# Turning the expert pairs' rows with VectorE's 32x32 blocks in place of TensorE transposes

## The chip, the cores and the metric

The kernel runs on one core of a Trainium2 chip. The metric is the device time of one execution in microseconds (us), as the median of three runs. One execution is also profiled; the profile gives each engine's instructions, waits and transfers. The engines are TensorE (PE, with its weight loads shown as PEld), VectorE (DVE), ScalarE (ACT), GpSimd (POOL) and SyncE (SP, which here only issues transfers).

## What is computed

The input is x, 64 batches of 256 rows with 256 columns, and a 256 x 256 adjacency mask that all batches share. Everything is fp32. Two layers follow one another:

```python
# layer 0
x = x + gat4(layernorm(x), adj, W0, a0)             # 4 heads of 64, softmax over masked neighbours, elu
x = x + layernorm(x) @ weight.T + bias
# layer 1
x = x + gat1(layernorm(x), adj, W1, a1)             # 1 head of 256, relu
t = layernorm(x)                                    # the expert layer gets t and also starts from it
out = t
for e in range(8):                                  # the two best of 8 experts have weights, others 0
    out = out + combine[:, e:e+1] * (gelu(t @ w1[e] + b1[e]) @ w2[e] + b2[e])
x = x + out
```

The router (softmax over 8 logits, the best two, weights made to sum to 1) makes `combine`.

## The kernel before

**Tiling.** A batch is two tiles of 128 rows. Each batch passes through 19 stages (`batch_layers`): attention of layer 0, its linear layer, attention of layer 1, the norm, and the router's logits. A matmul needs the features of its input on the partitions. So the input x is loaded twice: as rows (`xin`) and, for the first projection, as blocks (`xblk`, `load_blocks`) in such an order that one VectorE instruction, which turns every 32x32 block by itself, gives x transposed (line 472). Four transfers load one batch's blocks, one for each group of 32 partitions, in pieces of 32 columns (128 B).

**Experts.** For 62 of the 64 batches ("routed") only the two chosen experts are computed. After the router, `route` computes for each row and choice a place in a buffer in DRAM, `xs`, where every expert has a region; `send` (line 845) scatters the rows there with indirect transfers of GpSimd. A sent row has 260 numbers: 256 features, and 4 more that say to which row of the output it belongs, its first expert, and two numbers for its weight. Full groups of 256 rows of one expert are called pairs (two tiles). `expert_pair` handles one: it loads the rows (`xr`, line 703, one transfer of 128 pieces of 2,080 B) and the expert's first weights (`we`, line 714), turns the rows with four TensorE transposes (`px`, line 721), copies them from PSUM with ScalarE (`sT`, line 725), casts the output row's index to an integer (`to`, line 728) and makes the weight (`w`, lines 730 and 734). `hidden` is the first matmul and the gelu (`ph`, line 753; `hT`, line 759), `result` the second (`py`, line 768; `y`, line 774). ScalarE multiplies by the weight (line 746), and `scatter` (line 785) adds the rows to the output with two indirect transfers of GpSimd, each pair's behind those of the pair before. There are 131 pairs. The last two batches ("dense") get all eight experts.

**Order.** The program order on every engine is the order in which the Python code emits instructions; each engine works through its own instructions in that order. The code emits in steps. Three steps, called phases 0, 1 and 2 in the code, make one period, in which one new batch begins, so six or seven batches are in work at different stages. Every job (a batch, a pair, a scatter) is a generator. It emits one piece per step, and the number that it yields is the rank of its next piece: within a step, pieces are emitted by rising rank. A negative rank means a later place in the same step. In these texts "phase 2 of 3" or "second phase" is the step in which a period's pairs are turned (the code's phase 1), and the third phase is the one after it, in which the next batch begins. Around the change the pieces are:

| step | rank | piece |
|---|---|---|
| second phase | 20, 28 | first projection `pq` (line 365), scaled `q` (line 381) |
| | 25 | `pd`, `z` of layer 1 (lines 419, 424) |
| | 50 | attention of layer 0: `pv` (line 456), `rinv` (463), `hp` (491) |
| | 55 | `pt` of the normed rows (line 351) |
| | 60 | `x2 + rel` and its norm statistics (lines 537, 336, 337); the pair's `px`, `sT`, `to`, `w` |
| | 70 | `pf` (line 511), x2 (line 517) and its norm statistics |
| | 90 | for chunks of one or two batches: places of the rows (lines 880 to 907) |
| third phase | 5 | x1 (lines 500 to 503) |
| | 10 | `pd`, `z` of two heads (lines 435, 442) |
| | 30 | the pair's `hidden`: `ph` |
| | 35, 40 | logits `pl`; attention of layer 1 `pv` |

Batches are routed in chunks of four, later of two and one (`CHUNKS`). Two pairs begin per period on average while batches still come, and three at the end; in the chunks of four the counts go 3, 2, 2, 1. A pair's rows are loaded when the last row of its chunk has been sent.

All these loads are issued by SP in program order. PSUM is used as eight banks in turn (`bank`); `px` takes one for each pair.

Of the kernel before, what the change touches and what calls it, by code (L numbers as in the profile page):

```python
# [9 lines left out]
F32 = mybir.dt.float32  # L10
# [17 lines left out]
def kernel(  # L28
# [72 lines left out]
    def load_blocks(b):  # L101


        t = io.tile([P, KT, N], F32, tag="xblk", name=f"xblk_{b}", bufs=3)
        for g in range(P // S):
            nc.sync.dma_start(
                out=t[g * S : (g + 1) * S].rearrange("q k (c a) -> q k c a", a=S),
                in_=x[b].rearrange("(c q) (k g a) -> g q k c a", q=S, g=P // S, a=S)[g],
            )
        return t  # L110

    S = 32
    AHEAD, BLOCKS_AHEAD = 3, 2
# [40 lines left out]
    def gnn_weights(w, a, heads, slope, name):  # L154

        d = D // heads
        wx = const.tile([P, KT, heads, d + 3], F32, tag=name, name=name)
        for k in range(KT):
            nc.sync.dma_start(
                out=wx[:, k, :, :d],
                in_=w[k * P : (k + 1) * P, :].rearrange("p (h d) -> p h d", h=heads),
            )
        av = work.tile([P, 2, d], F32, tag="e", name=name + "_a", bufs=1)
        nc.scalar.dma_start(out=av.rearrange("p s d -> p (s d)"), in_=rows_to_all(a, 2 * d))
        flat = wx.rearrange("p k h c -> p k (h c)")  # L170
        return flat, lambda: score_columns(wx, av, heads, slope, name)
# [51 lines left out]
    def prepare_r():  # L223
        pr = bank("pr", [KT, E])
        for k in range(KT):
            nc.tensor.transpose(pr[:, k, :], r_in[:, k * P : (k + 1) * P], ident[:E, :E])
        nc.vector.tensor_copy(rT, pr)
# [9 lines left out]
    def pack_expert(e):  # L237
# [4 lines left out]
            in_=w1[e].rearrange("(k p) f -> p k f", p=P),  # L242
# [20 lines left out]
        fill[:, :, D : D + 1], pattern=[[1, 2], [1, 1]], base=(B - 1) * N, channel_multiplier=2,  # L263
        allow_small_or_imprecise_dtypes=True,
# [82 lines left out]
    def transposed(src, tag="xT", bufs=4):  # L347
        pt = bank("pt", [KT, N])
        for t in range(NT):
            for k in range(KT):  # L350
                nc.tensor.transpose(  # L351
                    pt[:, k, t * P : (t + 1) * P], src[:, t, k * P : (k + 1) * P], ident
                )
        dst = work.tile([P, KT, N], F32, tag=tag, name="xT", bufs=bufs)
        nc.scalar.copy(dst, pt)  # L355
        return dst
# [109 lines left out]
    def batch_layers(b, c0, xng, lg):  # L466
# [4 lines left out]
        xT = work.tile([P, KT, N], F32, tag="xT", name="xT", bufs=4)  # L471
        nc.vector.transpose(xT.rearrange("p k n -> p (k n)"), xb.rearrange("p k n -> p (k n)"))
# [99 lines left out]
        xT = transposed(xe[:, :, :D], *(("xTd", DENSE) if dense else ()))  # L572
# [115 lines left out]
    def expert_pair(j, n, ids, ef, regs, needs):  # L688
# [3 lines left out]
        if i == 0:  # L692
# [9 lines left out]
        xr = io.tile([P, 2, ROW], F32, tag="xr", name="xr", bufs=XBUFS)  # L702
        load = nc.sync.dma_start(
            out=xr,
            in_=xs_d.rearrange("(t p k) c -> t p k c", p=P, k=2)[
                bass.ds(t_sp, 1), :, :, :
            ].rearrange("t p k c -> (t p) k c"),
        )
        tc.add_to_no_dep_group("rows", load.ins)
        for name in needs:  # L710
            tc.add_manual_dep(load.ins, name, AFTER, reason="any sent row may lie in the pair")
# [5 lines left out]
        yield 60  # L717
        px = bank("px", [KT, PAIR])
        for t in range(2):
            for k in range(KT):  # L720
                nc.tensor.transpose(  # L721
                    px[:, k, t * P : (t + 1) * P], xr[:, t, k * P : (k + 1) * P], ident
                )
        xT = work.tile([P, KT, PAIR], F32, tag="sT", name="sT", bufs=3)
        nc.scalar.copy(xT, px)  # L725

        to = small.tile([P, 2], I32, tag="to", name="to", bufs=8)
        nc.vector.tensor_copy(to[:, :, None], xr[:, :, D : D + 1])  # L728
        w = small.tile([P, 2], F32, tag="w", name="w", bufs=8)
        nc.vector.scalar_tensor_tensor(  # L730
            w[:, :, None], xr[:, :, D + 1 : D + 2], ef[:, j : j + 1], xr[:, :, D + 2 : D + 3],
            op0=ALU.is_equal, op1=ALU.mult,
        )
        nc.vector.tensor_tensor(w[:, :, None], w[:, :, None], xr[:, :, D + 3 : D + 4], ALU.add)  # L734
        yield 30
        hT = hidden(xT, we)
# [10 lines left out]
        scatters.append((y, to))  # L747
# [31 lines left out]
    def scatter():  # L779

        y, to = scatters.pop(0)
        before = added[-2:] + based
        based.clear()
        for t in range(2):
            d = nc.gpsimd.indirect_dma_start(  # L785
                out=out_rows, out_offset=bass.IndirectOffsetOnAxis(ap=to[:, t : t + 1], axis=0),
# [75 lines left out]
    def route(c, row0, nt, n, last, xng, lg):  # L862
# [46 lines left out]
        r4 = rt([nt, 4], "r4")  # L909
        vec.tensor_scalar(r4[:, :, 0:1], token[:, :nt, None], float(row0), None, op0=ALU.add)  # L910
        vec.tensor_scalar(r4[:, :, 1:2], first[:, :, None], float(E), None, op0=ALU.add)
        two = two_weights(c, nt, ed)
        for k in range(2):
            vec.tensor_copy(r4[:, :, 2 + k : 3 + k], two[:, k, :, None])
        for i, xe in enumerate(xng):
            vec.tensor_copy(xe[:, :, D:], r4[:, i * NT : (i + 1) * NT, :])
# [169 lines left out]
```

## Time and profile before

| | |
|---|---|
| median of three runs | 1705.36 us (1704.01 to 1710.16) |
| profiled execution | 1703.31 us |
| its span, first to last instruction | 1701.6 us |
| mean granted TensorE clock | 0.966 |
| DMA packets | 272,541, of which 153,848 under 512 B |
| issued by SP: `xr` | 131 transfers of 260 KB |
| `we` | 147 of 288 KB |
| `xblk` | 256 of 64 KB |

Of a group of instructions the profile gives its line in the kernel, engine and operation, what is written and read, the count, then the engine's busy time and the mean duration of one, then the idle time of the engine just before such instructions and what ended it. A matmul's duration contains its pipeline; successive ones overlap, so the distance of their starts is what they cost. The idle time of an engine matters only where others wait for it.

### The profile page before, as it was taken

How to read it: one execution, taken by the hardware profiler on the slowest of the kernel's cores; microseconds unless marked ns; L12 is line 12 of the kernel's file. 1: busy time of each engine (PE TensorE's matmuls, PEld its weight loads, DVE VectorE, ACT ScalarE, POOL GpSimd, SP SyncE). 2: the span in 40 equal slices, each digit the busy share in tenths (PEclk: the TensorE clock that was granted, in tenths of full speed). 3: DMA queues.
4: the chain of work that ended last, by engine and by line, in shares of the span. 5: the costliest groups of instructions: out<-in, count | busy, mean ns of one | idle time of the engine just before them, and what ended most of it. 6: DMA issues, size and time to landing. Idle time of an engine off the chain costs nothing. (4 is left out here: it accounts for less than half of the span.)

```text
span 1701.6 us, 29737 instructions
## 1 busy us (share of the span) xinstructions
PE 1536.7 (90%) x8998; PEld 1352.9 (80%) x8998; DVE 1273.9 (75%) x4744; ACT 897.3 (53%) x1965; POOL 879.4 (52%) x790
## 2 busy tenths in 40 slices
PE   5898888899999999999999999999999997698792
PEld 4777777788888888888888888888888886587681
DVE  6888999988878888888888888878889977422221
ACT  0253434465666566656666665655556675433240
POOL 0122334446565665656565656565675656634444
PEclk8999999999999999999999999999999999889896
DMA  4822223345556564646565554555464555674653
GB/s 107 221 51 48 63 75 88 87 131 108 145 127 151 127 152 113 141 107 143 131 142 137 116 148 99 142 124 148 113 140 116 119 142 139 170 196 97 153 124 43
DMA packets 272541, 209.67 MB, mean 123 GB/s; under 512 B 153848, under 2 KB 226560, under 8 KB 272384
## 3 DMA queue, kind: packets, MB, share of 16 engines
q1 hardware_dynamic: 221760, 139.40, 29.6%
q0 software_dynamic: 49632, 67.39, 21.7%
q8 instruction: 74, 1.21, 0.3%
q10 hardware_dynamic: 992, 0.99, 0.2%
q14 instruction: 83, 0.68, 0.1%
HBM read 118.55 MB, written 89.15 MB: 122 GB/s over the span
## 5 line engine op out<-in xcount | busy, mean ns | idle before, releaser
L785 POOL DMA_INDIRECT out_dram<-y,to x262 | 416.2, 1589 | 318.9 <-DMA out_dram<-y,to 145.9
L456 PE MATMUL pv<-q,z 128*128 128x65 f32 (+1 forms) x2560 | 367.4, 298 | 3.6 <-issue 3.0
L456 PEld LDWEIGHTS pv<-q,z 128*128 128x128 f32 x2560 | 330.4, 193 | 15.5 <-issue 3.2
L344 POOL TENSOR_SCALAR rstd<-mv 128x4 f32<-128x4 f32 (+1 forms) x132 | 74.4, 564 | 415.9 <-DVE mv L337 314.4
L753 PE MATMUL ph<-sT,we 128*128 128x256 f32 x1048 | 248.7, 393 | 41.5 <-ACT sT L725 21.8
L845 POOL DMA_INDIRECT xs<-xng,pos x248 | 249.5, 1006 | 69.2 <-issue 67.1
L768 PE MATMUL py<-w2s,hT 128*128 (+1 forms) x1176 | 263.8, 379 | 0.5 <-PE pt L351 0.5
L753 PEld LDWEIGHTS ph<-sT,we 128*128 128x128 f32 x1048 | 202.4, 198 | 71.7 <-ACT sT L725 23.7
L768 PEld LDWEIGHTS py<-w2s,hT 128*128 128x128 f32 x1176 | 219.6, 190 | 28.6 <-PE pt L351 0.7
L355 ACT COPY xT<-pt 128x512 f32<-128x512 f32 x192 | 113.2, 590 | 234.4 <-PE pt L351 228.7
L774 DVE TENSOR_TENSOR y<-py,b2s 128x512 f32<-128x512 f32 x147 | 98.0, 689 | 162.1 <-PE py L768 101.6
L442 DVE SCALAR_TENSOR_TENSOR z<-pd,q,mask 128x256 f32<-128x256 f32 x512 | 211.2, 474 | 0.3 <-PE pd L435 0.2
L759 ACT ACTIVATE hT<-ph,we 128x256 f32<-128x256 f32 x294 | 123.5, 471 | 149.1 <-PE ph L753 101.0
L345 POOL TENSOR_TENSOR rstd<-rstd,mhalf 128x4 f32<-128x4 f32 (+1 forms) x132 | 160.2, 1214 | 11.0
L746 ACT ACTIVATE y<-y,w 128x256 f32<-128x256 f32 x262 | 113.0, 503 | 90.0 <-DVE y L774 86.7
L336 DVE BATCH_NORM_STATS2 stats<-x 128x6 f32<-128x256 f32 x384 | 156.4, 407 | 2.2
L365 PE MATMUL pq<-wx,xT 128*128 128x268 f32 x512 | 137.4, 414 | 8.3 <-DVE wt L239 4.2
L400 PE MATMUL pq<-wx,xT 128*128 128x259 f32 x512 | 129.2, 394 | 16.1 <-ACT xT L355 14.7
L400 PEld LDWEIGHTS pq<-wx,xT 128*128 128x128 f32 x512 | 91.9, 189 | 42.8 <-ACT xT L355 28.7
L365 PEld LDWEIGHTS pq<-wx,xT 128*128 128x128 f32 x512 | 100.8, 201 | 29.4 <-issue 6.9
L511 PE MATMUL pf<-wfT,xT 128*128 128x256 f32 x512 | 122.4, 382 | 1.0 <-issue 0.8
L533 ACT ACTIVATE rel<-pv,rinv 128x256 f32<-128x256 f32 x128 | 53.9, 474 | 110.9 <-DVE rinv L463 107.4
(155 smaller groups left out, 2393.4 us busy)
## 6 DMA issues: line engine op xcount, KB each, us to landing
we<-wpack SPq DMA_DIRECT2D x147, 288.0 KB
xr<-xs SPq DMA_DIRECT2D x131, 260.0 KB
xblk<-in_x_dram SPq DMA_DIRECT2D x256, 64.0 KB
xin<-in_x_dram SPq DMA_DIRECT2D x64, 256.0 KB
out_dram<-base SPq DMA_DIRECT2D x64, 256.0 KB
out_dram<-y,to POOLq DMA_INDIRECT x262
xs<-xng,pos POOLq DMA_INDIRECT x248
xs<-fill SPq DMA_DIRECT2D x9, 260.0 KB
```

Source lines behind the costliest of these rows:

```text
L336: nc.vector.bn_stats(stats[:, t, :], src[:, t, :])
L345: nc.gpsimd.tensor_tensor(rstd[:, :n], rstd[:, :n], mhalf[:, :n], ALU.pow)
L365: nc.tensor.matmul(pq.rearrange("p h c -> p (h c)"), xT[:, k, t * P : (t + 1) * P], wx[:, k, :], start=(k == 0), stop=(k == KT - 1),)
L400: nc.tensor.matmul(pq, xT[:, k, t * P : (t + 1) * P], wx1[:, k, :], start=(k == 0), stop=(k == KT - 1),)
L442: nc.vector.scalar_tensor_tensor(z[:, j, :], pd[:, i, :], q[:, j, h, d + 2 : d + 3], mask[:, j, :], op0=ALU.max, op1=ALU.mult,)
L456: nc.tensor.matmul(pv[:, h, :], z[:, j, t * P : (t + 1) * P], q[:, j, h, : d + 1], start=(j == 0), stop=(j == NT - 1),)
L511: nc.tensor.matmul(pf[:, t, :], xT[:, k, t * P : (t + 1) * P], wfT[:, k, :], start=(k == 0), stop=(k == KT - 1),)
L753: nc.tensor.matmul(ph[:, f, :], we[:, k * D + f * P : k * D + (f + 1) * P], xT[:, k, :], start=(k == 0), stop=(k == KT - 1),)
L759: nc.scalar.activation(hT[:, f, :], ph[:, f, :], AF.Gelu, bias=we[:, C_B1 + f : C_B1 + f + 1])
L768: nc.tensor.matmul(py[:, t, :], hT[:, f, t * P : (t + 1) * P], w2s[:, e, f * D : (f + 1) * D].rearrange("p e c -> p (e c)"), start=(f == 0 ...
L785: d = nc.gpsimd.indirect_dma_start(out=out_rows, out_offset=bass.IndirectOffsetOnAxis(ap=to[:, t : t + 1], axis=0), in_=y[:, t, :], in_off ...
L845: d = nc.gpsimd.indirect_dma_start(out=xs_d[: E * CAP * PAIR, :], out_offset=bass.IndirectOffsetOnAxis(ap=at, axis=0), in_=xe, in_offset=None,
```

## The change

The rows of `xs` are loaded as blocks too. Feature f no longer lies at partition f mod 128 of half f div 128: partition p now holds the features 2p and 2p + 1. So a group of 32 partitions gets 64 neighbouring columns (256 B) of each row; VectorE's turn then reads every second number. The same order of features is used for the input's blocks and for the router's input, and the rows of the weights `W0`, the router and `w1` are loaded to match.

For each pair SP issues five transfers in place of one: four of 32 rows x 8 pieces of 256 B, and a fifth for the four extra numbers of each row, into a tile `xt` of its own with 12 buffers. The piece with the `px` transposes, the ScalarE copy, the cast and `w` at rank 60 is gone. In its place, at rank 95 of the same step, stands one VectorE turn (`turned`); `w` is made behind `hidden`, at rank 65 of the next step. The index of the output row is now stored as an integer when the row is made, so the cast isn't needed; that takes one small instruction per batch in `route`.

```diff
-        t = io.tile([P, KT, N], F32, tag="xblk", name=f"xblk_{b}", bufs=3)
+        t = io.tile([P, N // S, KT * S], F32, tag="xblk", name=f"xblk_{b}", bufs=3)
         for g in range(P // S):
             nc.sync.dma_start(
-                out=t[g * S : (g + 1) * S].rearrange("q k (c a) -> q k c a", a=S),
-                in_=x[b].rearrange("(c q) (k g a) -> g q k c a", q=S, g=P // S, a=S)[g],
+                out=t[g * S : (g + 1) * S],
+                in_=x[b].rearrange("(c q) (g f) -> g q c f", q=S, g=P // S)[g],
             )
...
+    def turned(dst, blocks):
+        nc.vector.transpose(
+            dst.rearrange("p k (c q) -> p k c q", q=S),
+            blocks.rearrange("p c (a k) -> p k c a", k=KT),
+        )
+        return dst
+    def by_block(ap):
+        return ap.rearrange("p (a k) -> p k a", k=KT)
...
-            nc.tensor.transpose(pr[:, k, :], r_in[:, k * P : (k + 1) * P], ident[:E, :E])
+            nc.tensor.transpose(pr[:, k, :], by_block(r_in)[:, k], ident[:E, :E])
...
-            in_=w1[e].rearrange("(k p) f -> p k f", p=P),
+            in_=w1[e].rearrange("(p k) f -> p k f", p=P),
...
-        xT = work.tile([P, KT, N], F32, tag="xT", name="xT", bufs=4)
-        nc.vector.transpose(xT.rearrange("p k n -> p (k n)"), xb.rearrange("p k n -> p (k n)"))
+        xT = turned(work.tile([P, KT, N], F32, tag="xT", name="xT", bufs=4), xb)
...
-        xT = transposed(xe[:, :, :D], *(("xTd", DENSE) if dense else ()))
+        xT = transposed(xe[:, :, :D], *(("xTd", DENSE) if dense else ()), blocks=True)
...
-        xr = io.tile([P, 2, ROW], F32, tag="xr", name="xr", bufs=XBUFS)
-        load = nc.sync.dma_start(
...
+        xr = io.tile([P, PAIR // S, KT * S], F32, tag="xr", name="xr", bufs=XBUFS)
+        loads = [
+            nc.sync.dma_start(
+                out=xr[g * S : (g + 1) * S],
+                in_=xs_d.rearrange("(t c q) f -> t q c f", c=PAIR // S, q=S)[
+                    bass.ds(t_sp, 1), :, :, g * KT * S : (g + 1) * KT * S
+                ].rearrange("t q c f -> (t q) c f"),
+            )
+            for g in range(P // S)
+        ]
+        xt = small.tile([P, 2, ROW - D], F32, tag="xt", name="xt", bufs=12)
+        loads.append(
+            nc.sync.dma_start(
+                out=xt,
+                in_=xs_d.rearrange("(t k p) c -> t p k c", p=P, k=2)[
+                    bass.ds(t_sp, 1), :, :, D:
+                ].rearrange("t p k c -> (t p) k c"),
+            )
+        )
...
-        yield 60
-        px = bank("px", [KT, PAIR])
-        for t in range(2):
-            for k in range(KT):
-                nc.tensor.transpose(
-                    px[:, k, t * P : (t + 1) * P], xr[:, t, k * P : (k + 1) * P], ident
-                )
-        xT = work.tile([P, KT, PAIR], F32, tag="sT", name="sT", bufs=3)
-        nc.scalar.copy(xT, px)
-
-        to = small.tile([P, 2], I32, tag="to", name="to", bufs=8)
-        nc.vector.tensor_copy(to[:, :, None], xr[:, :, D : D + 1])
+        yield 95
+        xT = turned(work.tile([P, KT, PAIR], F32, tag="sT", name="sT", bufs=3), xr)
         w = small.tile([P, 2], F32, tag="w", name="w", bufs=8)
-        nc.vector.scalar_tensor_tensor(
...
         yield 30
         hT = hidden(xT, we)
+        yield -65
+        nc.vector.scalar_tensor_tensor(
+            w[:, :, None], xt[:, :, 1:2], ef[:, j : j + 1], xt[:, :, 2:3],
+            op0=ALU.is_equal, op1=ALU.mult,
+        )
+        nc.vector.tensor_tensor(w[:, :, None], w[:, :, None], xt[:, :, 3:4], ALU.add)
         yield 80
...
-                out=out_rows, out_offset=bass.IndirectOffsetOnAxis(ap=to[:, t : t + 1], axis=0),
+                out=out_rows, out_offset=bass.IndirectOffsetOnAxis(
+                    ap=xt[:, t, 0:1].bitcast(I32), axis=0
+                ),
...
         for i, xe in enumerate(xng):
-            vec.tensor_copy(xe[:, :, D:], r4[:, i * NT : (i + 1) * NT, :])
+            vec.tensor_copy(xe[:, :, D + 1 :], r4[:, i * NT : (i + 1) * NT, :])
+            vec.tensor_scalar(
+                xe[:, :, D : D + 1].bitcast(I32), token[:, i * NT : (i + 1) * NT, None],
+                float(row0), None, op0=ALU.add,
+            )
```

## The prediction

> **What bounds the kernel now.** I read four views in this order: the page, the busy time by stage, the groups by line, and the timeline of one steady period. The page, then three stages of the table by stage (columns: length, busy us and instructions of PE, PEld, DVE, ACT, POOL, granted clock, DMA share, GB/s):
>
> ```profile
> PE 1536.7 (90%) x8998; PEld 1352.9 (80%) x8998; DVE 1273.9 (75%) x4744; ACT 897.3 (53%) x1965; POOL 879.4 (52%) x790
> ...
> 500.00:600.00 100.00, 98.31 (x608) 88.16 (x608) 79.72 (x289) 60.47 (x129) 62.04 (x54) 1.00 0.56 127
> 1200.00:1300.00 100.00, 93.99 (x554) 83.46 (x553) 84.19 (x348) 58.39 (x125) 63.44 (x58) 0.97 0.55 133
> 1500.00:1600.00 100.00, 79.91 (x373) 69.50 (x373) 24.96 (x72) 33.87 (x77) 43.71 (x28) 0.90 0.59 131
> ```
>
> From about 340 to 1390 us TensorE is the bound (94 to 98%), VectorE close behind, DMA at little over half. The groups that the change touches:
>
> ```profile
> L721 PE MATMUL px<-ident,xr 128*128 128x128 f32 x524 | 70.3, 276 | 8.8 <-DMA xr<-xs 7.0 <-DVE rinv L463 0.9 <-DVE q L381 0.8
> L725 ACT COPY sT<-px 128x512 f32<-128x512 f32 x131 | 70.6, 598 | 10.4 <-PE px L721 10.3
> L472 DVE STREAM_TRANSPOSE xT<-xblk 128x512 f32<-128x512 f32 x64 | 45.0, 704 | 0.0
> L728 DVE CAST to<-xr 128x2 int32<-128x2 f32 x131 | 22.1, 169 | 9.2 <-DMA out_dram<-y,to 8.9 <-issue 0.3
> ```
>
> Then the stretch where the pairs' rows are turned, in a period with two pairs, PE first and then DVE (start, length, what):
>
> ```profile
> 635.49 3.68 PE L456 MATMUL pv<-q,z 128*128 128x65 f32 x32
> 639.01 0.60 PE L351 MATMUL pt<-ident,xng 128*128 128x128 f32 x4
> 639.45 1.04 PE L721 MATMUL px<-ident,xr 128*128 128x128 f32 x8
> 640.32 1.89 PE L511 MATMUL pf<-wfT,xT 128*128 128x256 f32 x8
> 642.05 0.60 PE L435 MATMUL pd<-ident,q 128*128 128x128 f32 x4
> 642.49 3.62 PE L753 MATMUL ph<-sT,we 128*128 128x256 f32 x16
> ```
>
> ```profile
> 639.21 0.18 DVE L463 RECIPROCAL rinv<-pv 128x4 f32<-128x4 f32 x1 [1.42 <-PE pv L456]
> 639.31 0.72 DVE L491 TENSOR_TENSOR hp<-pv,rinv 128x256 f32<-128x256 f32 x2
> 639.95 0.68 DVE L537 TENSOR_TENSOR x<-x,rel 128x512 f32<-128x512 f32 x1
> ...
> 641.76 0.14 DVE L728 CAST to<-xr 128x2 int32<-128x2 f32 x1
> ...
> 642.56 0.87 DVE L517 SCALAR_TENSOR_TENSOR x<-pf,rstd,x1b 128x256 f32<-128x256 f32 x2
> ...
> 644.43 0.66 DVE L500 SCALAR_TENSOR_TENSOR x<-hp,xin 128x512 f32<-128x512 f32 x1
> ```
>
> Call T the end of the pv matmuls, 635.49 + 3.68 = 639.17. PE needs only T+3.32 to reach ph, and has no gap in between. VectorE, which starts its work of this step when pv is there, ends it with the second phase's last work at T+5.26 (L500 is the next phase's first). So PE is 1.94 us ahead of VectorE here. Today that costs nothing, since ph takes sT from ScalarE.
>
> **What the Trainium skill says.** "VectorE: DVE Perf Modes", The three transpose paths: VectorE turns 32x32 blocks only, TensorE a whole 128x128 into PSUM. The trace has both: 704 ns for a 128x512 block turn, 276 ns for a PE transpose, though eight of them pass in 0.87 us (639.45 to 640.32). "SBUF — State Buffer", Door 1: at a stride of two fp32, two accesses still share a 16-byte line and keep full bandwidth; no strided turn or PE transpose is in this trace. "DMA: Bandwidth & Descriptors", Why a DMA increments its semaphore by 16: a descriptor moves one contiguous run; the 131,072 runs of 128 B of xblk fit the 153,848 packets under 512 B on the page. "TensorE: Matmul & The Clock Gate", Why this matters for your kernels: idle gaps over about 3 us halve the clock. The trace agrees at its ends: after gaps of 3.3 us (from 150 and 223 us) the granted clock was 0.50 for 3 to 7 us, after 2.2 us (1419) it stayed 1.00.
>
> **The change, part by part.**
>
> PE loses the px transposes: 0.87 us for two pairs, 0.44 a pair. ACT loses 131 copies of 598 ns; at 53% busy they are worth nothing, ph's start excepted.
>
> VectorE loses the cast and moves the two w instructions: both pairs' six ran from 641.76 to 642.56, 0.80 us, out of this stretch. The w part (220 + 163 ns a pair) goes behind ph in the third phase; there VectorE has waits on py and pd of over 1 us a period that cover it; without them, 0.7 us a period.
>
> VectorE gains a turn per pair, 704 ns by L472. Its source now has a stride of two fp32: between 0.70 (kept, by the page above) and twice that. This holds for L472 too, and for the PE transposes of xng (0.44 us a batch, up to 0.88). I take no penalty; twice as long, the turn costs 0.7 us in each of the 46 periods below, 32 us, and the transposes 28.
>
> Where the turn stands decides. Its rank is 95 in phase 2 of 3, behind L517 and its two norm statistics (rank 70), ahead of L500 (rank 5 of the next step). ph has rank 30 of that next step, and only pd (rank 10) lies before it on PE. VectorE without the 0.80 us finishes at 644.43 - 0.80 = 643.63 (L517 doesn't wait: pf then ends at 641.34, before 641.76). One turn: 644.33. With about 0.05 us of handing over, ph starts at T+5.2. PE is ready at 3.32 - 0.87 = T+2.45. It stands for 2.7 us, and all of PE behind ph with it: pl, the next pv, py, the next batch's pq. The 0.87 saved is inside this wait. If the rows are late, the turn itself waits, and behind it on VectorE L500 to L503 and the z's of the next scores, for which ScalarE, GpSimd's norms and PE's next transposes wait in turn. Net: 5.2 - 3.32 = +1.9 us for a two-pair period. The loop closes on itself: the next T follows ph by PE's own work (661.75 on the timeline, 19.3 us later, 0.24 us of it waiting), and the next turn follows T. VectorE's total isn't the limit: about 80% of a period, plus two turns less two casts, 1.1 us.
>
> Periods come in fours with 3, 2, 2, 1 pairs. One pair: ph at T+2.88 now (593.24), at least T+5.2 then, +2.3; VectorE starts there 2 us late today, which may stay in part. Three pairs: T+4.56 now (612.34, with 0.6 us of waiting for rows), T+5.2 then, +0.6, more if DMA is late. Sum at the least 0.6 + 1.9 + 1.9 + 2.3 = 6.7; I take 7.5 per four periods, the late starts weighed in. From 340 to 1138 us there are 35 periods, 8.75 fours: **+66 us**.
>
> From 1138 to 1375 us the chunks are of one or two batches, and their routing puts about 2.5 us of small VectorE work (both to pos, 1168.05 to 1170.55) at rank 90 of phase 2, ahead of the turn. There are 11 periods, eight with such a block: 8 x (5.2 + 2.5) and 3 x 5.2, a mean of 7.0, against 4.1 now on the timeline: 11 x 2.9 = **+32**.
>
> Clock: a gap of 2.7 us lies between the 2.2 that kept it and the 3.3 that didn't. Halving costs about 1.4 us (24 ph took 6.86 us at 1443.67 against 5.43 at 1399). Ends: none, or all 46 periods at 1.4 to 1.7, 65 to 78. I take the eight long gaps only: **+11**.
>
> DMA: a pair's load of 128 runs becomes 1,024 of 256 B and 256 of 16 B, five issues on SP instead of one; xblk's runs halve in number. On SP's timeline one of 128 runs takes 0.34 us, of 256 runs 0.40 (out from base), of 512 0.63. Four more at about 0.5 with their address: 2 us a pair, while SP waits 12.8 us a time (564.6 us in 44 waits) for sent rows. Two-pair loads are issued 11 us before their use: hidden. In three-pair periods xr was issued at 607.23, 5.1 us before T; fifteen issues take 7.5 us, and the we loads behind them reach SP at T+2.5 and, with the 3.35 us that the chain shows for we, land at T+6. That is under 1 us beyond the turn, inside the 7.5; at 0.75 us an issue it is 4 us.
>
> The rest: one more 0.17 us VectorE instruction per batch in a stretch where it waits for q, hidden, else 7 us in all. The weights' row order and the integer index change no count that repeats. In the tail the turn stands behind the last y (0.69) and base (0.88) where px took 1.33 us: about +1 us in three or four rounds, partly under the 6.4 us a pair of the scatter chain: **+2**.
>
> Sum: 66 + 32 + 11 + 2 = +111 on the profiled execution's 1703.3 us, which is 2 us under the median of 1705.4: about **1815 us**.
>
> **Rivals.** (a) The turn is ready before PE arrives, and PE's saving counts: 95 pairs are turned before 1390 us (380 px transposes in the table by stage) x 0.44 = 42, about 1661 us. It decides if the first turn ends before T+2.45; the timeline says 5.2. Chance 0.06. (b) The turn in effect falls where the cast stood: T+2.6+0.7 = T+3.3, as now, so about 1705. Ranks speak against it. 0.04. (c) Clock halves in nearly every period: 66 to 78 us in place of 11, about 1875. The gap is short of 3.3. 0.12. (d) SP can't issue fast enough: rows and we late by 4 us in each four periods, and VectorE's queue stands behind the turn: 11 x 4 more, about 1859. For it: the 0.6 us wait for rows today. 0.12. Main case 0.66, own range 1757 to 1850: the low end lets the wait swallow all of PE's present idle time (2.8% of the 90.7 us of four periods, 2.5 us, so 6.7 - 2.5 = 4.2 x 8.75 = 37) and takes half the 32 and no clock.
>
> Cases (a) and (b) lie outside below 1750, half of (c) above 1875. Within 0.5% is about what a measurement tells from no change: faster 0.06, same 0.03, slower 0.91.
>
> **What would show it.** In the changed trace: PE idle of 2 to 3 us before ph, released by VectorE's turn; the turn straight before L500; the distance T to ph at 5 us or more with two pairs; PE's share in the steady stages falling from 97 to about 90%; ACT's busy time 70 us lower. Wrong if ph follows pd without a gap, if the wait is put down to DMA of xr or we, or if the turn takes well over 0.7 us.

## The result and the profile after

The changed kernel takes 1849.86 us (median of 4 runs, 1844.06 to 1855.46), beside 1707.76 us of the kernel before on the same chip. The ratio is 1.083, with a 95% interval from 1.078 to 1.088: the change costs about 142 us. The profiled execution took 1844.06 us, with a span of 1842.3 us.

The page's line of busy times, and then the three stages shown of before (columns as there):

```profile
PE 1539.8 (84%) x8474; PEld 1338.9 (73%) x8474; DVE 1358.5 (74%) x4786; ACT 830.2 (45%) x1834; POOL 856.0 (46%) x790
...
500.00:600.00 100.00, 87.53 (x501) 76.92 (x500) 78.48 (x265) 50.85 (x113) 52.73 (x48) 0.97 0.55 119
1200.00:1300.00 100.00, 83.39 (x479) 73.34 (x478) 82.00 (x316) 46.44 (x101) 52.07 (x48) 0.95 0.48 108
1500.00:1600.00 100.00, 74.59 (x357) 64.52 (x356) 63.24 (x299) 50.22 (x108) 58.39 (x52) 0.86 0.62 131
```

TensorE has 524 instructions fewer, and yet is busy for 3 us more. In the steady stage its share fell from 98 to 88%, and no other engine's rose: nothing is the bound by its busy time any more. The groups say who makes whom wait (the first line is from before):

```profile
L753 PE MATMUL ph<-sT,we 128*128 128x256 f32 x1048 | 248.7, 393 | 41.5 <-ACT sT L725 21.8 <-DMA we<-wpack 19.7
L779 PE MATMUL ph<-sT,we 128*128 128x256 f32 x1048 | 301.9, 453 | 208.2 <-issue 99.4 <-DVE sT L116 72.0 <-DVE posf L933 11.2
L116 DVE STREAM_TRANSPOSE xT<-xblk 128x512 f32<-128x512 f32 x64 | 45.0, 703 | 0.0
L116 DVE STREAM_TRANSPOSE sT<-xr 128x512 f32<-128x512 f32 x131 | 84.6, 688 | 0.0
```

TensorE stood 208 us ahead of `ph`, against 41.5 us before. "Issue" here is a gap for which the profile names no releaser; the timeline below shows what ends just then. The turn itself costs 688 ns, with no idle time ahead of it: its rows are there when VectorE comes to it. Here are a two-pair period on PE and then on DVE, the same stretch as shown of before:

```profile
705.94 3.68 PE L476 MATMUL pv<-q,z 128*128 128x65 f32 x32
709.46 0.68 PE L369 MATMUL pt<-ident,xng 128*128 128x128 f32 x4
709.98 1.89 PE L530 MATMUL pf<-wfT,xT 128*128 128x256 f32 x8
711.70 0.60 PE L455 MATMUL pd<-ident,q 128*128 128x128 f32 x4
714.94 3.69 PE L779 MATMUL ph<-sT,we 128*128 128x256 f32 x16 [2.63 <-issue]
```

```profile
709.66 0.18 DVE L483 RECIPROCAL rinv<-pv 128x4 f32<-128x4 f32 x1 [1.23 <-PE pv L476]
709.76 0.72 DVE L510 TENSOR_TENSOR hp<-pv,rinv 128x256 f32<-128x256 f32 x2
710.40 0.68 DVE L556 TENSOR_TENSOR x<-x,rel 128x512 f32<-128x512 f32 x1
...
712.21 0.84 DVE L536 SCALAR_TENSOR_TENSOR x<-pf,rstd,x1b 128x256 f32<-128x256 f32 x2
...
714.13 1.30 DVE L116 STREAM_TRANSPOSE sT<-xr 128x512 f32<-128x512 f32 x2
715.35 0.65 DVE L519 SCALAR_TENSOR_TENSOR x<-hp,xin 128x512 f32<-128x512 f32 x1
```

T, the end of pv, is 709.62. VectorE works without a pause from T to the turn. The first of the two turns starts at T+4.50, lasts 0.71 us, and `ph` starts at T+5.32. TensorE has ended its `pd` at T+2.7.

In the rest of this document the steady stretch is the 35 periods from 340 us on (349 us in the changed kernel) whose chunks have four batches, and a "four" is four of them in a row, with 3, 2, 2 and 1 pairs. Figures for a four are from the third to the seventh of a run, about 520 to 1,050 us. A four took 90.8 us before and takes 99.2 us now.

### The profile page after: what moved, and what is told of

Same layout as the page of the kernel before. It is cut to its first block, busy times and chain, and to the rows that moved or that the text cites. A ratio compares the mean times of both kernels' runs of the same rounds, so it can differ in the third digit from the quotient of the medians.

```text
span 1842.3 us, 30415 instructions
## 1 busy us (share of the span) xinstructions
PE 1539.8 (84%) x8474; PEld 1338.9 (73%) x8474; DVE 1358.5 (74%) x4786; ACT 830.2 (45%) x1834; POOL 856.0 (46%) x790
## 4 chain that ended last, share of the span: by engine, by line
PE 60%; DVE 18%; issue 10%; DMA 5%; SPq 3%; ACT 2%; POOL 2%; DVEq 0%; POOLq 0%; ACTq 0%
PE ph L779 17%; PE pv L476 13%; PE py L794 11%; PE pq L385 5%; PE pq L420 5%; DVE stats L354 3%; PE pf L530 3%; PE pt L369 3%; DVE z L462 2%; PE pl L596 2%; SPq L723 2%; DVE mv L355 1%; DMA out_dram<-y,xt 1%; DMA we<-wpack 1%; PE pd L455 1%
## 5 line engine op out<-in xcount | busy, mean ns | idle before, releaser
L811 POOL DMA_INDIRECT out_dram<-y,xt x262 | 416.2, 1589 | 241.7 <-issue 62.1
L779 PE MATMUL ph<-sT,we 128*128 128x256 f32 x1048 | 301.9, 453 | 208.2 <-issue 99.4
L779 PEld LDWEIGHTS ph<-sT,we 128*128 128x128 f32 x1048 | 237.0, 231 | 263.9 <-issue 156.7
L362 POOL TENSOR_SCALAR rstd<-mv 128x4 f32<-128x4 f32 (+1 forms) x132 | 41.4, 314 | 657.1 <-DVE mv L355 542.7
L873 POOL DMA_INDIRECT xs<-xng,pos x248 | 259.3, 1046 | 69.1 <-issue 66.7
L385 PE MATMUL pq<-wx,xT 128*128 128x268 f32 x512 | 141.9, 425 | 8.3 <-DVE wt L257 4.2
L363 POOL TENSOR_TENSOR rstd<-rstd,mhalf 128x4 f32<-128x4 f32 (+1 forms) x132 | 143.2, 1085 | 11.0
L483 DVE RECIPROCAL rinv<-pv 128x4 f32<-128x4 f32 (+1 forms) x256 | 40.3, 168 | 114.3 <-PE pv L476 90.6
L420 PEld LDWEIGHTS pq<-wx,xT 128*128 128x128 f32 x512 | 91.8, 189 | 44.0 <-ACT xT L375 24.9
```

Source lines behind the costliest of these rows:

```text
L363: nc.gpsimd.tensor_tensor(rstd[:, :n], rstd[:, :n], mhalf[:, :n], ALU.pow)
L385: nc.tensor.matmul(pq.rearrange("p h c -> p (h c)"), xT[:, k, t * P : (t + 1) * P], wx[:, k, :], start=(k == 0), stop=(k == KT - 1),)
L420: nc.tensor.matmul(pq, xT[:, k, t * P : (t + 1) * P], wx1[:, k, :], start=(k == 0), stop=(k == KT - 1),)
L779: nc.tensor.matmul(ph[:, f, :], we[:, k * D + f * P : k * D + (f + 1) * P], xT[:, k, :], start=(k == 0), stop=(k == KT - 1),)
L811: d = nc.gpsimd.indirect_dma_start(out=out_rows, out_offset=bass.IndirectOffsetOnAxis(ap=xt[:, t, 0:1].bitcast(I32), axis=0), in_=y[:, t, ...
L873: d = nc.gpsimd.indirect_dma_start(out=xs_d[: E * CAP * PAIR, :], out_offset=bass.IndirectOffsetOnAxis(ap=at, axis=0), in_=xe, in_offset=None,
```

## The experiments

The question was what of the change costs the time: where the turn stands on VectorE (my theory), a slower turn, or the transfers in pieces and their five issues on SP. All kernels are small edits of the kernel before or of the changed kernel. The table has the median, the ratio to the kernel before in the same comparison, a four, and the distance from T to the first `ph` in the periods of 3, 2 and 1 pairs of these five fours (us).

| kernel | median | ratio (95%) | a four | T to ph: 3, 2, 1 pairs |
|---|---|---|---|---|
| before | 1707.8 | 1 | 90.8 | 4.0 to 4.9, 3.3, 2.9 to 3.1 |
| changed | 1849.9 | 1.078 to 1.088 | 99.2 | 5.3, 5.3, 5.3 |
| input blocks alone | 1709.9 | 0.997 to 1.001 | 91.0 | 4.0 to 5.5, 3.3, 2.9 to 3.1 |
| turn, one transfer | 1845.3 | 1.078 to 1.084 | 99.4 | 5.2, 5.2, 5.2 to 5.5 |
| pieces, turned on PE | 1800.1 | 1.047 to 1.055 | 98.9 | 13.0 to 14.0, 3.3, 2.9 |
| turn at rank 60 | 1805.6 | 1.050 to 1.060 | 99.8 | 4.8 to 9.5, 3.5, 5.3 to 5.6 |
| turn at rank 45 | 1787.1 | 1.043 to 1.048 | 97.3 | 9.5 to 10.6, 2.5 to 3.2, 2.5 to 2.9 |
| statistics behind the turn | 1758.9 | 1.026 to 1.032 | 93.1 | 4.15 in all |
| `we` first, before | 1747.2 | 1.015 to 1.022 | 93.9 | 6.8 to 9.4, 3.3, 2.9 |
| `we` first, rank 60 | 1761.4 | 1.021 to 1.030 | 95.7 | 3.5 to 3.7, 3.5, 5.5 to 6.1 |
| and later turns in the wait | 1721.5 | 1.004 to 1.009 | 92.2 | 5.6 to 6.8, 2.5, 2.5 to 3.3 |
| same, one transfer | 1714.6 | 1.003 to 1.007 | 90.8 | 5.5 to 6.6, 2.5, 2.5 to 2.7 |
| staggered 45, 60, 95 | 1718.7 | 1.005 to 1.010 | 89.8 | 2.8 to 4.0, 2.5, 2.5 to 2.8 |
| staggered 45, 52, 60 | 1688.2 | 0.988 to 0.992 | 88.5 | 2.8 to 3.6, 2.5, 2.5 to 3.2 |

### The input's blocks alone

The kernel before with only the 64-column blocks of x, the turn with its stride of two numbers, and the rows of `W0` to match.

> The kernel before with one part of the change alone: the input's blocks in pieces of 64 columns, the turn at L472 with a stride of two numbers, and W0's rows to match. The pairs are as before. Theory A: the same time as before within 0.5%, 1700 to 1712 us; the turn stays at 0.70 us, SP's issues of xblk fall from 0.63 to about 0.45 us, and PE doesn't notice. Theory C (a strided turn is slow): L472 goes well over 0.7 us, and the time rises by up to 0.7 us per batch, 45 us.

No change was measured. With the 703 and 688 ns of the strided turns above, against 704 before, a slower turn is excluded. "SBUF — State Buffer", Door 1, from which I had argued that a stride of two fp32 keeps the bandwidth, agrees with this for VectorE.

It does not carry over to TensorE. The transposes of the normed rows (`pt`) read with the same stride in the changed kernel, and their weight loads, before and after, are:

```profile
L351 PEld LDWEIGHTS pt<-ident,xng 128*128 128x128 f32 x256 | 30.8, 156 | 1.3 <-issue 0.8 <-ACT xng L551 0.4
L369 PEld LDWEIGHTS pt<-ident,xng 128*128 128x128 f32 x256 | 37.8, 216 | 0.1
```

The starts of the four transposes of a batch span 0.39 us in place of 0.33, and from the first to the next matmul it is 0.51 us in place of 0.44 (medians). In the runs made from the kernel before, this one included, `pt` has no stride and it stays 0.44. The prediction took no penalty for it; it is 0.07 us a batch.

### The turn without the issues, and the pieces without the turn

Two kernels take the change apart; the second of them ran first. In the first the changed kernel's four row transfers are one, with as many packets of the same size. In the second the kernel before gets the pieces and `xt`, and turns them on TensorE as ever (its `xt` has the rows in another order than the changed kernel's, and an issue of it takes 572 ns in place of 390).

```diff
-            for g in range(P // S)
...
+        loads = [
+            nc.sync.dma_start(
+                out=xr,
+                in_=xs_d.rearrange("(t c q) w -> t c (q w)", c=PAIR // S, q=S)[
+                    :, :, : P * KT * S
+                ].rearrange("t c (p f) -> t p c f", p=P)[
+                    bass.ds(t_sp, 1), :, :, :
+                ].rearrange("t p c f -> (t p) c f"),
+            )
+        ]
```

> The changed kernel with the four transfers of a pair's rows put into one: the same 1024 packets of 256 bytes and the same 256 KB, but one issue on SP instead of four, so that the tokens' numbers lie in other places than the pair's own (the hidden layers are computed from misplaced numbers; every other instruction has its size). It is the turn on VectorE without the pieces' issues; the run with the pieces turned on TensorE was the pieces without the turn, and cost 87 us. Theory A (the turn's place on VectorE alone costs the time of the change, and in the changed kernel the issues are hidden by it): T to ph stays at 5.3 us in every steady period, four periods at 99.0 us, time 1835 to 1855. Theory B (the issues on SP cost it): four periods fall to about 91 us, 1700 to 1730. If both add up in part: 1750 to 1820.

> The kernel before, with the pair's rows fetched as in the changed kernel (four pieces of 64 columns and the routing columns apart, five issues on SP instead of one, 256-byte packets), but turned on TensorE through the identity and copied by ScalarE as before. TensorE turns the 512 elements of each partition as they lie, so that the pairs' hidden layers are computed from misplaced numbers; every instruction has its size. It takes the transfers without the turn on VectorE. My theory (the place of the turn on VectorE costs the time; the transfers are hidden behind the periods): within 1.5% of before, 1700 to 1735. Theory B (the pieces and their issues cost the time): 1780 to 1850, with waits of px for xr or of ph for we.

The turn alone took 1845.3 us: the whole time of the change. So in the changed kernel the four issues cost nothing that can be measured. But the pieces alone took 1800.1 us, and there I was wrong: I had expected 1700 to 1735, and theory B's 1780 to 1850 came out. Its timeline shows a period of three pairs, on PE and then on SP (T is 835.92):

```profile
836.65 0.63 PE L736 MATMUL px<-ident,xr 128*128 128x128 f32 x4 [0.29 <-PE pt L351]
840.10 1.08 PE L736 MATMUL px<-ident,xr 128*128 128x128 f32 x4 [2.83 <-DVE stats L336]
844.90 1.09 PE L736 MATMUL px<-ident,xr 128*128 128x128 f32 x4 [3.71 <-DMA xr<-xs]
845.78 3.62 PE L511 MATMUL pf<-wfT,xT 128*128 128x256 f32 x8
```

```profile
830.95 4.40 SPq L704 DMA_DIRECT2D xr<-xs  x4
835.40 0.62 SPq L714 DMA_DIRECT2D xt<-xs  x1
836.26 1.96 SPq L704 DMA_DIRECT2D xr<-xs  x4
838.41 0.61 SPq L714 DMA_DIRECT2D xt<-xs  x1
839.30 2.45 SPq L704 DMA_DIRECT2D xr<-xs  x4
841.94 0.57 SPq L714 DMA_DIRECT2D xt<-xs  x1
```

A chunk's first three pairs can be fetched only once its last rows have been sent, at T-5.3, and then SP has fifteen issues to make. They last from T-5.0 to T+6.6. TensorE reaches the second and the third `px` before their rows and stands in front of each; its `pf` waits behind them. (The profile puts the second wait down to VectorE's statistics, for which `px` doesn't wait in the kernel before; the last packets of these rows end at about 839.6.) In periods of one and two pairs the distances are those of the kernel before. That it is the issues and not the small packets is read from the trace, since no run turned the pieces on TensorE with one transfer: a packet of 256 B takes 18 ns (median), so the 1,024 of a pair take about 1.2 us on 16 DMA engines (an estimate from the trace), while the five issues of a pair take 2.8 to 5.1 us here. Why some of the first pair's issues stand 1.45 us apart is open.

So there are two limits, and each alone makes a four of about 99 us. They don't add up: in the changed kernel the second is covered by the first. Here are its issues on SP in a period of three pairs (T is 853.56):

```profile
843.31 2.93 SPq L723 DMA_DIRECT2D xr<-xs  x4
846.96 0.01 SPq L734 DMA_DIRECT2D xt<-xs  x1
847.69 1.54 SPq L723 DMA_DIRECT2D xr<-xs  x4
849.50 0.39 SPq L734 DMA_DIRECT2D xt<-xs  x1
850.09 2.86 SPq L723 DMA_DIRECT2D xr<-xs  x4
853.14 0.39 SPq L734 DMA_DIRECT2D xt<-xs  x1
```

The sends are issued at T-14.6 to T-10.3, not at T-9.2 to T-5.3, and the fifteen row issues run from T-10.2 to T, in most such periods to T-1. That TensorE's T has moved back by its own standing, while the sends have not, is how I read this; only the times are measured. The first period of three pairs speaks for it. There TensorE hasn't yet stood in period after period; the fifteen run from T-5.5 to T+3.7, as late as with the pieces alone, and `ph` starts only at T+8.85.

### The turn earlier

Two ranks that put the turn ahead of L536 (60: behind the first statistics; 45: ahead of `rinv`), and an edit that leaves it at its rank and emits the statistics of L536's x2 behind it.

```diff
-        yield 95
+        yield 60
```

> The changed kernel with the turn at rank 60 of the second phase, where the old copies stood, ahead of L517 and its statistics. Theory A (the place of the turn on VectorE sets when ph starts): with two pairs the turn ends about 2.6 + 0.7 us behind the end of pv, so ph starts at T+3.3 as in the kernel before, the 2.6 us idle time of PE before ph shrinks to about 0.7, and the time goes back to about that of before: 1700 to 1730 us. Theory B (the small pieces and the five issues of SP hold the pairs up): the place changes little, and the time stays above 1820. Theory C (the block turn with a stride itself is slow, or the halved clock is the cause by itself): also above 1820.

> The turn at rank 45 of the second phase, ahead of rinv, so it falls into VectorE's wait of 1.2 to 1.4 us for pv. Theory A: where the rows are there in time ph follows pd without a gap, T+2.7; that saves 0.44 us per pair against before, about 1665 us. But in three-pair periods the fifteen issues end only about T-1 and land 3 us later, so the turn and all of VectorE behind it would wait for rows; if that happens in one period of four at some 4 us, the gain is eaten: 1690 to 1720. Theory B: such waits of VectorE on the transfers are large and frequent and the time lies above 1760.

```diff
+        yield -96
         _, rstd = norm_stats(x2)
```

> The changed kernel with the norm statistics of x2 (two statistics and two aggregates, 1.1 us) moved from ahead of the turn to behind it, still in the second phase; the turn stays behind L517. Theory A: ph starts 1.1 us earlier, at about T+4.2 with two pairs, in each of the 46 periods, and the shorter gap halves the clock less often: 50 to 70 us less than the changed kernel, about 1790. Theories B and C: no change, 1840 to 1850.

At rank 60 the two-pair periods did what my theory says: `ph` at T+3.48, 1.84 us earlier. The kernel was still 95 us above the kernel before, between what the theories had said. In periods of one pair VectorE itself was late: it had waited for ScalarE's `q`, and its `rinv` starts at T+1.9, as the first lines show (T is 822.86). The kernel before has the same lateness there (T+2.2 to T+2.8); its cause was not followed up. The second fence, from the waits of the run with rank 45 (total, times, longest), belongs to the periods of three:

```profile
823.93 0.88 DVE L401 SCALAR_TENSOR_TENSOR q<-pq,rstd,q 128x256 f32<-128x256 f32 x2 [3.29 <-ACT q L393]
824.73 0.24 DVE L483 RECIPROCAL rinv<-pv 128x4 f32<-128x4 f32 x2
...
827.49 0.71 DVE L116 STREAM_TRANSPOSE sT<-xr 128x512 f32<-128x512 f32 x1
```

```profile
PE ph L779 <- DMA we<-wpack: 79.7, 12, 19.8
...
DVE sT L116 <- DMA xr<-xs: 32.4, 24, 2.6
```

With the turn out of the way the wait went to the loads: `we`, issued behind fifteen row transfers, came last. At rank 60 that is 56 us in 11 waits, of which seven lie in the nine steady periods of three pairs, 2.2 to 6.8 us each. (The expectation of the run with `we` first, below, has 14 us in 11 waits; 14 us is the longest of them.) At rank 45 it is 80 us in 12 waits, five of them in those periods, about 7 to 8 us each; there the turns also wait for their rows, with VectorE's queue behind them. A four fell only to 97.3 us, and the time, 1787.1 us, is what theory B had said.

The two statistics and their aggregates take 1.1 us (713.0 to 714.1 in the DVE timeline above). A two-pair period with them behind the turn (T is 768.58):

```profile
770.66 0.60 PE L455 MATMUL pd<-ident,q 128*128 128x128 f32 x4
772.73 3.69 PE L780 MATMUL ph<-sT,we 128*128 128x256 f32 x16 [1.47 <-issue]
```

```profile
771.93 1.29 DVE L116 STREAM_TRANSPOSE sT<-xr 128x512 f32<-128x512 f32 x2
773.15 0.38 DVE L354 BATCH_NORM_STATS2 stats<-x 128x6 f32<-128x256 f32 x1
```

`ph` starts at T+4.15 in place of T+5.32, in every steady period but the first. The steady stretch became 61.2 us shorter, of which T to `ph` is 45.1 (191.2 to 146.1). The other 16 fit the clock: at gaps of 1.47 us no half-clock window is left there, where the changed kernel has 41 us of them. For the whole I had said 50 to 70 us less, some of it by the clock, and got 91 (1758.9 us). T to `ph` gives 58 of them, 13 in the small chunks included; the rest, more than I had allowed for the clock, fits it but was not taken apart.

### The order of the loads, and VectorE's own wait

`we` is loaded ahead of the rows, and `xt` one step later; then (`yield 60 if j < 3 else 26` in place of the last line) the turns of all pairs but a chunk's first three go into VectorE's wait for `q`; and, as a control, `we` first in the kernel before.

```diff
+        we = io.tile([P, WROW], F32, tag="we", name="we", bufs=WBUFS)
+        nc.sync.dma_start(
+            out=we, in_=wpack[bass.ds(e_sp, 1), :, :].rearrange("e p c -> (e p) c")
+        )
         xr = io.tile([P, PAIR // S, KT * S], F32, tag="xr", name="xr", bufs=XBUFS)
...
         yield 90
+        xt = small.tile([P, 2, ROW - D], F32, tag="xt", name="xt", bufs=12)
...
-        yield 95
+        yield 60
```

> The changed kernel with three edits: the turn at rank 60, the load of we issued ahead of the pair's rows, the load of xt (the routing columns) moved to the step at rank 90, behind the rows. With the turn at rank 60 alone the four periods took 99 to 100 us: the two-pair periods fell to 3.48 us from T to ph, but in the period of three pairs ph waited for we (14 us in 11 waits), and in the period of one pair VectorE came 1.8 to 2.1 us late. Theory A (issue order on SP is what was left in the three-pair periods): the waits for we vanish, ph in three-pair periods comes 3.5 to 4.5 us after T, four periods fall to about 96 us, time about 1760. Theory B (the transfers themselves are late, whatever the order): the wait moves from we to the rows (sT<-xr late), four periods stay at 99 us, time 1795 to 1815. The late VectorE in the one-pair period stays in both.

> As the run with we first, and the turns of every pair but a chunk's first three run at rank 26, that is inside VectorE's wait for ScalarE earlier in the period, instead of at rank 60. If VectorE's order is all that costs time once the loads come in time, ph follows T by 2.5 to 3.5 us in every steady period, the half-clock windows go, four periods take 88 to 90 us and the time is 1670 to 1700, less than before the change. If transfers or SP's issues still hold the rows back, the earlier turns wait for their rows and hold VectorE's queue: four periods of 97 us or more, time 1780 or more.

> The kernel before with the load of we issued ahead of the pair's rows, nothing else: a control for the order of the two loads. SP has two issues per pair here and none waits late, so no change: within 0.5% of before, 1700 to 1720. If the order itself matters (rows then late for the turn on TensorE), 1720 to 1750.

The first came out as theory A had it (1761.4; three pairs at T+3.48). With the later turns at rank 26 nearly all other periods reach T+2.51, which is when TensorE is ready: no gap is left there. The time, 1721.5, lies between what the two theories gave; what remained was a gap of 2.9 us in the periods of three pairs. The control missed what I expected first; the 1720 to 1750 for the case that the order itself matters held. In the kernel before the new order costs 1.9%, not nothing. There, in periods of three pairs, the second and the third pair's rows are issued 2.2 to 2.3 us later, behind `we`s of 288 KB, and `px` waits for them (2.44 us in the period looked at), with `pf`, `pd` and `ph` behind it. The order of loads isn't free where TensorE has the rows to turn.

### Which order is left

The same kernel with one transfer for the rows ("the run before this one" is the turn with one transfer, above), and two other orders of the first three turns of a chunk.

> The run with we first and the later pairs' turns inside VectorE's wait, with the four transfers of the rows put into one as in the run before this one (numbers misplaced in the same way). Both limits are taken away at once. If the two are all that the change costs, ph follows T by 2.5 us in periods of one and two pairs and by 4.8 to 5.6 us in those of three (there the turns stand behind the statistics), four periods take 89 to 92 us, time 1665 to 1710. If the packets themselves are the limit (1024 of 256 bytes a pair), the rows stay late and it takes 1720 or more.

```diff
-        yield 60 if j < 3 else 26
+        yield (45, 60, 95)[j] if j < 3 else 26    # the last kernel: (45, 52, 60)
```

> The run with we first and the later pairs' turns inside VectorE's wait, with the first three pairs of a chunk turned at ranks 45, 60 and 95 instead of all at 60: the first turn goes ahead of rinv and the statistics, the third behind them. There the period of three pairs was what remained: ph 5.58 us after T, a gap of 2.9 us, one half-clock window, and a third turn that waited 1.1 us for its rows with VectorE's queue behind it. If the order on VectorE is what is left, ph follows T by 2.8 to 3.3 us in those periods too, the half-clock windows go, four periods take 87 to 89 us and the time is 1675 to 1695, less than before the change. If the rows of the first pair land too late for it (they are issued from 5 us ahead of T), ph stays at 4.5 us or later and the time at 1710 to 1730.

> The staggered kernel with a chunk's first three pairs turned at ranks 45, 52 and 60 instead of 45, 60 and 95: the second turn stands right behind hp, the third behind the statistics at rank 60 and ahead of L536 and of the routing arithmetic. With ranks 45, 60 and 95 the four periods took 89.8 us, and in the period of three pairs TensorE still stood 1.36 us ahead of the second pair's ph and 0.55 us ahead of the third's, 3.0 us where the routing arithmetic came between. If those turns are what is left, both gaps shrink to 0.5 us or less, four periods take 87.5 to 88.5 us and the time is 1680 to 1697, less than before the change. If the rows of the second and third pair are not there so early (their last issues are at 0 and 2.5 us after T), the turns wait for them with the statistics queued behind, and it takes 1705 to 1730.

With one transfer in place of four the ratio is 1.005 beside 1.006, with overlapping intervals, and the time just misses the 1710 that I had given: over the whole kernel the issues cost little here. In the two profiled executions the steady stretch was 8 us shorter with one transfer and the tail 7 us longer, which was not followed up. Staggering 45, 60, 95 closed the first gap and opened others. Its timeline, TensorE in a period of three pairs:

```profile
795.20 1.97 PE L782 MATMUL ph<-sT,we 128*128 128x256 f32 x8
798.52 1.99 PE L782 MATMUL ph<-sT,we 128*128 128x256 f32 x8 [1.36 <-DVE mv L355]
801.06 1.99 PE L782 MATMUL ph<-sT,we 128*128 128x256 f32 x8 [0.55 <-DVE sT L116]
```

The first pair's `ph` comes at once, the second's and third's stand. Its expected 1675 to 1695 was missed by 24 us: where the routing arithmetic lies between the second and the third turn (chunks of one or two batches), the third `ph` waited 3.0 us. With 45, 52 and 60 (page's line, then TensorE in a period of three pairs):

```profile
PE 1508.8 (89%) x8474; PEld 1313.9 (78%) x8474; DVE 1344.1 (80%) x4786; ACT 835.7 (50%) x1834; POOL 879.4 (52%) x790
```

```profile
786.55 0.60 PE L455 MATMUL pd<-ident,q 128*128 128x128 f32 x4
787.27 3.87 PE L782 MATMUL ph<-sT,we 128*128 128x256 f32 x16
792.27 1.99 PE L782 MATMUL ph<-sT,we 128*128 128x256 f32 x8 [1.13 <-DVE sT L116]
794.10 0.95 PE L596 MATMUL pl<-rT,xT 128*128 128x8 f32 x8
```

The first two pairs go through; the third stands 1.13 us, where I had said 0.5 or less, since its turn waits 0.63 us for its rows. A four takes 88.5 us and the kernel 1688.2 us: 1.0% less than before the change (0.8 to 1.2%), and about 9% less than the changed kernel (1688.2 / 1849.9 = 0.913, from two comparisons). It has the change's transfers and its turn on VectorE; only the order of turns and loads is another. In the 35 steady periods T to `ph` sums to 91.8 us, 32.9 less than before; the 0.44 us of TensorE that each pair saves make 31 for 71 pairs. The steady stretch itself became 24.3 us shorter (798.2 to 773.9 us), since the third pair's `ph` still stands. So in this stretch most of the saving is on the path at last. Outside it the kernel takes 9 us more than before: 4.9 in the small chunks and 4.2 ahead of 340 us.

## Why the prediction was right

Predicted were 1815 us (1750 to 1875) and slower with 0.91; measured were 1849.9. The spans of the two profiled executions differ by 140.7 us, and the sum of the prediction has 111. By its own terms:

| term | predicted | measured |
|---|---|---|
| 35 steady periods: `ph` later after T | 66 | 66.5 |
| 10 periods with small chunks: the same | 32 | 30.7 |
| clock, in both stretches | 11 | 25.9 (what is left) |
| ahead of 340 us, and the tail | 2 | 8.8 + 8.8 |

The measured values of the first two rows are sums of T to `ph`: 124.7 us before and 191.2 after in the steady stretch, 41.9 and 72.6 in the other. The prediction counted 11 periods in the latter; 10 end in it. That 66 was met so closely has luck in it: the periods at T+5.32 give 61, and the other 5 are from the first two periods of three pairs, with `ph` at T+8.85 and T+6.98. The prediction's allowance of 0.8 us a four (7 us) was for another thing, late starts of VectorE.

**The mechanism.** It was the one forecast, step by step: VectorE ends L536 and its statistics, turns, and only then L519 follows; `ph` at T+5.32 where 5.2 was said; a gap of 2.6 us where 2.7 was said; TensorE's share at 88% where about 90% was said; ScalarE 67 us less busy where 70 was said. That VectorE no longer comes late at T in periods of one and three pairs (`rinv` at T+0.04) was half said: late starts were weighed in, and there are almost none. TensorE is ready at T+2.51 where 2.45 was said, about what the stride of its `pt` costs (0.07 us).

**The clock** was mis-sized. I took it to halve in eight long gaps only. In the steady stretch it shows 41 us at half speed in eleven windows, before none; in the other 44.4 us against 6.8. What the two stretches lost beyond T to `ph` is 81.6 - 66.5 = 15.1 and 41.5 - 30.7 = 10.8 us. This remainder was not taken apart; that it is the clock fits: in windows at half speed TensorE loses at most half their length, 20.5 and 18.8 us. I knew that 2.2 us had kept the clock and 3.3 us had not, and put 2.7 on the safe side; it was neither, since the length of a gap alone does not decide (last section).

**The ends.** A pair is turned ahead of 340 us too: its `ph` went from T+2.88 to T+6.32, and the clock shows 51.2 us at half speed there against 30.7. The tail has 100.1 us at half speed against 79.6, and half of the difference, 10 us, would cover its 8.8. I had counted instructions at the ends, and no gaps.

**The hidden loads.** "Two-pair loads are hidden" held, and that the three-pair loads lie inside the 7.5 us held in the changed kernel, but not for the reason I gave. I let the fifteen issues start at T-5.1, as before. They start at T-10.2. I gave rival (d) 4 us a four at 0.75 us an issue. Uncovered, an issue does take 0.75 us on average (about 10.5 us for the fourteen steps from the first to the last), but a four then takes 8.1 us more, with the turn on TensorE. As long as the turn stands at rank 95 this is hidden; once the turn comes early, it is what ends last. The prediction treated (d) as an addition; it is an alternative.

**The other rivals.** (a), the turn ready before TensorE, is possible, but only with another order of turns and loads, and gave 1688.2 us where 1661 was said. (b), the turn where the cast stood, is nearly the run with rank 60: two-pair periods at T+3.48, and yet 1806 us, since it left out what comes next. (c), the clock halved in nearly every period, holds in the small chunks only (eight windows in ten periods); in the steady stretch it is eleven in 35. The main case's own range, 1757 to 1850, holds the measured median by 0.1 us, which is luck: two of the four runs lie above it. The terms that missed by much all missed upwards, and they are the clock and the ends.

## What to carry to other kernels

When work is moved to another engine, its place in that engine's order can cost more than its length: here a turn of 0.7 us, moved by nothing but its rank, made the difference between 1850 and 1787 us, and together with the loads' order that between 1850 and 1688 us. Two late things that wait for the same instruction hide one another, so an edit that cures one shows little, and an experiment that does one part alone can cost nearly as much as the whole. Look therefore at every kind of period (three, two, one pairs) separately, at what ends last in each, and cure them all before judging the idea.

## What the runs showed of the hardware

- In all fourteen traces the granted clock changes only on a grid of 3.413 us steps. From 340 us to the end, a full-clock step in which TensorE ran no matmul for 2.0 us or more was followed by a step at half clock in 255 cases of 255; of the 4,947 with less idle time 33 were, and why these is open. So a gap counts by how the grid cuts it. The prediction's gap of 2.2 us is cut into 0.36 and 1.89 us and kept the clock.
- In the changed kernel the gap ahead of `ph` is 2.64 us in every kind of period. From 655 us on a four takes 99.0 us, which is 29 steps, so the grid cuts each four alike: the gap of the three-pair period puts 2.0 to 2.1 us into one step, and a half-clock step follows (761.2, 860.2, 959.2 us and so on); the other three put at most 1.99 us into one, and none follows. Earlier, where the fours were longer, three of five windows came after gaps of two-pair periods. Gaps of 1.47 us brought none. "TensorE: Matmul & The Clock Gate", Why this matters for your kernels, has the halving at idle gaps over about 3 us; here 2.0 us within one step were enough.
- VectorE's fp32 32x32 turn of 128x512 has one price with and without a stride of two numbers in its source: 704 ns without, 688 to 703 with it. TensorE's weight load of a 128x128 fp32 block has two: 156 ns without, 216 with it (means over `pt`).
- On SP, an issue of a pair's load followed the one before it by 0.54 us in the changed kernel (median). Over the fifteen of a period with three pairs the mean is 0.62 to 0.70 us there, and 0.75 to 0.79 us in the pieces' run (the fours of the table). By itself the issue of a piece with 256 packets lasted 317 ns, and that of the single transfer with all 1024 packets 384 ns (medians). Issues are paid by the piece more than by the packet.
